# Attention of the last layer: other products take turns in the maxima's banks, q and k come in pieces of 256 tokens, polar pieces are dealt evenly

## The chip, the core and the metric

The kernel runs on one core of one Trainium2 chip. The time is device microseconds (us) of one execution. Five engines work side by side and meet at semaphores: TensorE (PE: matmuls, with its weight loads shown apart as PEld), VectorE (DVE), ScalarE (ACT), GpSimd (POOL) and SyncE (SP, which here only issues DMAs). Each runs its own instructions in the order in which the program gives them. PE writes its results to PSUM; the pools of this kernel divide it into eight banks of 128 x 512 float32.

## The reference

The program is a four-layer network over 2 sequences of 2048 tokens with 256 features. The change touches only the last layer:

```python
xn = _layernorm(x, axis=-1)
x = x + _L3_attn_ref(xn, Wq, Wk, Wv, Wo) + _L3_ffn_ref(xn, theta, phi, theta_noise, phi_noise)

# _L3_attn_ref: causal softmax attention, 16 heads of 16 features
scores = jnp.einsum('bhtc,bhkc->bhtk', q, k) * scale
scores = jnp.where(causal, scores, -jnp.inf)
attn = jax.nn.softmax(scores, axis=-1)
out = jnp.einsum('bhtk,bhkc->bhtc', attn, v)
return jnp.einsum('bsv,dv->bsd', out, o_proj_weight)

# _L3_ffn_ref ("polar"): length of a complex product
real = jnp.einsum('bti,io->bto', x, jnp.cos(theta + theta_noise))
imag = jnp.einsum('bti,io->bto', x, jnp.sin(phi + phi_noise))
return jnp.sqrt(real * real + imag * imag)
```

All of it is float32.

## The kernel before

The last layer is `layer3_attn`, with the polar part of sequence 0 done ahead of it by `layer3_ffn`. The 2 x 16 heads are cut into eight **groups** of four heads. A head has 16 features and takes a strip of 32 rows of the array, so that four heads' score matmuls stand in the four row strips together; a float32 matmul call shows in the profile as two matmul instructions. Each group goes through two passes over its scores. The *maxima pass* (`gm`, line 1380) computes q against k with queries on the partitions, and DVE takes the row maximum of each head (line 1401). The maxima are folded into a spare row of q (`fold`, lines 1234, 1240, 1242). The *exponential pass* (`ge`, line 1376) computes the scores again, transposed, with the maximum already subtracted; ACT takes the exponential (line 1390), POOL cuts the diagonal (1394), and PE multiplies by the values (1430, tile `ps_v`). `divide` scales by the row sums and `prod` multiplies by the output weights.

The order is written by hand, under a manual schedule. `waves` runs 40 **units** (tiles of 128 x up to 512 scores; 28 are 512 wide, four each 384, 256 and 128). It is called nine times:

- once for the maxima of group 0 alone (the *first maxima stage*),
- seven times for the exponentials of group n with the maxima of group n + 1 (the *joint stages*),
- once for the exponentials of group 7 alone (the *last stage*).

In a joint stage a unit consists of two **waves**; each has two score matmuls and two maxima matmuls, interleaved, e m e m. The value product of a unit ("held") is issued after the first wave of the next unit. In the other two stages a unit is one wave with all four heads, and a tile holds two heads in two banks.

Other work is put between units. `fill` is a list of steps in fixed order; `pieces` are products that become ready after a number of waves (`fold`'s transposes, `over` and `prod` of `divide`, the values of sequence 1); `steps` are the same without PE. After each unit (in a joint stage, after its second wave) one ready piece is taken, or else one fill step; and when as many fill steps are left as units, further ones are taken at once.

In the first maxima stage fill holds 53 steps. They are: values of sequence 0 (16), the polar part of sequence 1 in four blocks (for each: `stats` on ACT; `normed` on DVE and ACT; two `turned` transposes; four `product`s), and q and k of group 1 (8). With 53 steps and 40 units, 14 of them are taken at unit 0.

`qk` makes q and k of a group in four pieces of 512 tokens. A piece is two fill steps (`half`), one for each half of the 256 features; after the second, ACT copies the bank twice (line 1193 into the staging tile `qk`, which has one buffer; line 1194 into `qT`), and four DMAs on SP's queue (line 1196) move k's rows to their partitions in `kT`. For group 0 this runs bare, ahead of the first maxima stage.

The banks, eight in all:

| stage | banks before |
|---|---|
| first maxima stage | values 1 (`ps_v`, unused yet), other products 1 (`ps_p`), polar 2 (`ps_x`), maxima 2 double tiles (`ps_s`) |
| joint stages | `ps_v` 1, `ps_p` 1, scores 3 (`ps_e`), maxima 3 (`ps_m`) |
| last stage | `ps_v` 1, `ps_p` 1, scores 3 double tiles (`ps_s`) |

`f_tile` gives the one bank of `ps_p` to q and k, values, folds, `over` and `prod`. Line 68 is the helper `mm`, so that its products are told apart by their tiles (`ps_p<-w3b,xT` values, `ps_p<-w3b,se` output products, `ps_x<-cs,xT` polar products; line 1469 makes the polar transposes).

Of the kernel before, what the change touches and what calls it, by code (L numbers as in the profile page):

```python
# [14 lines left out]
F32 = mybir.dt.float32  # L15
# [8 lines left out]
P = 128  # L24
# [1077 lines left out]
def layer3_attn(g, tc, a, out):  # L1102
# [11 lines left out]

    nc = g.nc
    NQ = S // P
    with ExitStack() as es:
        wk = es.enter_context(tc.tile_pool(name="l3a", bufs=2))
        wb = None
        psv = es.enter_context(tc.tile_pool(name="l3v", bufs=1, space=bass.MemoryType.PSUM))  # L1120
        psf = es.enter_context(tc.tile_pool(name="l3p", bufs=1, space=bass.MemoryType.PSUM))
# [34 lines left out]
        def f_tile():  # L1156
            return psf.tile([P, 512], F32, name="ps_p", tag="f")
# [23 lines left out]
        def qk(G):  # L1181

            def half(n, k, st):
                def go():
                    if k == 0:
                        st["ps"] = f_tile()
                    nc.tensor.matmul(st["ps"], wqk[:, k, G.hg * P : (G.hg + 1) * P],  # L1187
                                     g.xT[:, k, G.b * S + n * 512 : G.b * S + (n + 1) * 512],
                                     start=k == 0, stop=k == 1)
                    if k == 1:  # L1190
                        c = slice(n * 512, (n + 1) * 512)
                        both = wk.tile([P, 512], F32, name="qk", tag="qk", bufs=1)
                        nc.scalar.copy(both, st["ps"])
                        nc.scalar.activation(G.qT[:, c], st["ps"], AF.Copy, scale=low16)
                        for j in range(4):
                            nc.sync.dma_start(G.kT[32 * j : 32 * j + 16, c], both[32 * j + 16 : 32 * j + 32, :])
                go.goes_on = k == 1
                return go

            fs = []  # L1200
            for n in range(4):
                st = {}
                fs += [half(n, 0, st), half(n, 1, st)]
            return fs
# [135 lines left out]
        def score_banks(both):  # L1340

            if both:
                pe3 = sc.enter_context(tc.tile_pool(name="l3e", bufs=3, space=bass.MemoryType.PSUM))
                pm3 = sc.enter_context(tc.tile_pool(name="l3m", bufs=3, space=bass.MemoryType.PSUM))
                return (lambda: pe3.tile([P, 1, 512], F32, name="ps_e3", tag="e"),
                        lambda: pm3.tile([P, 1, 512], F32, name="ps_m3", tag="m"))
            p2 = sc.enter_context(tc.tile_pool(name="l3s", bufs=3, space=bass.MemoryType.PSUM))
            return (lambda: p2.tile([P, 2, 512], F32, name="ps_s", tag="s"),) * 2

        def waves(ge, gm, fill, e_tile, m_tile):  # L1350
# [9 lines left out]
            for u in range(len(ue)):  # L1360
# [7 lines left out]
                for wave, (he, hm) in enumerate([((0, 1), (2, 3)), ((2, 3), (0, 1))] if both  # L1368
                                                else [((0, 1, 2, 3),) * 2]):
                    step = 1 if both else 2  # L1370
                    te = [e_tile() for _ in he[::step]] if ge else []
                    tm = [m_tile() for _ in hm[::step]] if gm else []
# [41 lines left out]

                    left = len(ue) - u
                    ready = [n for n, (when, f) in enumerate(pieces) if when <= now]
                    if ready and not (fill and (getattr(fill[0], "goes_on", False) or both and len(fill) >= left)):
                        pieces.pop(ready[0])[1]()
                    elif fill:
                        fill.pop(0)()  # L1420
                    while fill and len(fill) >= left:
                        fill.pop(0)()
                if ge:
                    def held(qb=qb, pts=pts, kt=kt, c0=c0):
                        nonlocal av
                        first, last = kt == 4 * qb, kt == (4 * qb - 1 if qb else 3)
                        if first:
                            av = psv.tile([P, 512], F32, name="ps_v3", tag="v")
# [12 lines left out]
        def polar(b):  # L1441

            fs = []
            for n in range(4):
# [3 lines left out]
                def stats(xb=xb, st=st):  # L1448
                    mv = st["mv"] = F.wk.tile([P, 3, 4], F32, name="mv3", tag="mv3")
# [41 lines left out]
        with tc.manual_schedule():  # L1491
            gs = [group(0), group(1)]
            for f in qk(gs[0]):
                f()
# [186 lines left out]
```

## Time and profile before

| | |
|---|---|
| median of 3 runs | 4361.61 us (4360.21 to 4363.71) |
| the profiled execution | 4356.61 us, its span 4354.9 us |
| PE busy | 3928.4 us, 90% of the span |
| DVE, ACT, POOL busy | 2544.0, 1954.2, 1278.9 us |
| bare q and k of group 0 | 2996.0 to 3012.2 us from the span's start |
| first maxima stage | 3012.2 to 3158.9 us |
| seven joint stages | 3158.9 to about 4240 us, some 154.4 us each |
| last stage and end | about 4240 to 4354.9 us |

The stages are read from the first and last starts of lines 1380 and 1376. In a line of a timeline the numbers are the start, in us from the span's start, and the duration; then engine, line, operation, and output tile <- input tiles, the shapes, and how many instructions were merged; in brackets stands the idle time of the engine before it and what ended it. In a line of the waits stand who waited, for whom, us in total, times, and the longest. The granted clock is the share of PE's full clock that the chip allowed in a stretch.

### The profile page before, as it was taken

To read this page: it belongs to the slowest core of one execution; us is meant where nothing else is said; L and a number is where in the kernel's file an instruction comes from. 1 tells how busy PE (TensorE), PEld (TensorE's weight loads), DVE (VectorE), ACT (ScalarE), POOL (GpSimd) and SP (SyncE) were. 2 spreads that over 40 slices of the span, in tenths; PEclk is the share of its full clock that TensorE was granted. 3 is DMA by queue.
4 is the path that set the end of the run, shared out by engine and by line. 5 is a ranking of instruction groups with operands and counts; after the bars stand their busy time and mean duration, and the time that the engine had idled before them with its cause. 6 is when DMAs were issued, how large, how long until landed. Compare 5 with 4: busy or idle time off the path is not lost.

```text
span 4354.9 us, 58086 instructions
## 1 busy us (share of the span) xinstructions
PE 3928.4 (90%) x21260; PEld 2297.7 (53%) x21260; DVE 2544.0 (58%) x6485; ACT 1954.2 (45%) x3713; POOL 1278.9 (29%) x1302
## 2 busy tenths in 40 slices
PE   6488988989879999999959999996999999999998
PEld 5356666766645555566536777673333333333332
DVE  6354444454378998999963322324666666666660
ACT  3234433343345555665422322324255555555556
POOL 1402222232166766656641111112111111101101
PEclk8687999999989999999979999998999999999999
DMA  4200222222345666666750000000000000000000
GB/s 179 91 32 32 73 70 79 79 79 80 128 119 186 219 199 208 212 211 216 223 180 1 1 1 1 1 1 25 4 8 8 5 4 16 16 9 9 4 2 26
DMA packets 106703, 330.18 MB, mean 76 GB/s; under 512 B 28561, under 2 KB 56866, under 8 KB 100018
## 3 DMA queue, kind: packets, MB, share of 16 engines
q0 software_dynamic: 52720, 264.15, 19.1%
q1 hardware_dynamic: 51234, 59.41, 4.2%
q8 instruction: 168, 2.75, 0.3%
q10 hardware_dynamic: 2464, 2.91, 0.2%
q14 instruction: 117, 0.96, 0.1%
HBM read 286.56 MB, written 33.03 MB: 73 GB/s over the span
## 4 chain that ended last, share of the span: by engine, by line
PE 53%; DVE 8%; DMA 3%; issue 2%; POOL 2%; ACT 1%; SPq 0%; ACTq 0%; DVEq 0%; POOLq 0%
PE ps_e L1376 12%; PE ps_v L1430 6%; PE ps_a L68 6%; PE ps_f L68 6%; PE ps_c L68 4%; PE ps_m L1380 3%; PE ps_k L68 2%; PE ps_p L68 2%; DMA G<-in_tab_in,ind 2%; PE ps_h L839 1%; DVE hid L817 1%; PE ps_o L1019 1%; PE ps_p L1187 1%; PE ps_s L1380 1%; PE ps_m L1384 1%
## 5 line engine op out<-in xcount | busy, mean ns | idle before, releaser
L1401 DVE TENSOR_REDUCE mp<-ps_m 128x1 f32<-128x512 f32 (+3 forms) x1120 | 632.1, 606 | 405.0 <-PE ps_m L1380 235.1
L1390 ACT ACTIVATE pt<-ps_e 128x512 f32<-128x512 f32 (+3 forms) x1120 | 537.9, 532 | 451.0 <-PE ps_m L1380 266.0
L1380 PE MATMUL ps_m<-kT,qT 32*128 32x512 f32 (+3 forms) x2240 | 677.2, 571 | 0.0
L1376 PE MATMUL ps_e<-qT,kT 32*128 32x512 f32 (+3 forms) x2240 | 656.0, 571 | 0.8 <-DVE mp L1401 0.5
L1376 PEld LDWEIGHTS ps_e<-qT,kT 32*128 32x128 f32 x2240 | 221.5, 183 | 354.9 <-issue 151.5
L1394 POOL TENSOR_SCALAR_AFFINE_SELECT pt<-pt 128x256 f32<-128x256 f32 x256 | 104.2, 408 | 857.6 <-ACT pt L1390 857.4
L805 POOL DMA_INDIRECT G<-in_tab_in,ind x256 | 273.8, 1070 | 213.8 <-DVE ind L792 63.8
L1430 PE MATMUL ps_v<-pt,vv 128*32 128x512 f32 (+3 forms) x2560 | 311.9, 541 | 1.6 <-POOL pt L1394 0.9
L805 POOL DMA_INDIRECT G<-in_tab_out,ind x256 | 268.1, 1047 | 85.5 <-issue 32.5
L68 PE MATMUL ps_e<-xgT,we 128*128 128x256 f32 x936 | 240.8, 404 | 27.0 <-ACT xgT L306 17.4
L68 PE MATMUL ps_f<-hb,l_b 128*128 128x512 f32 x1024 | 258.3, 404 | 0.0
L68 PE MATMUL ps_k<-wk,xt 128*128 128x512 f32 x512 | 255.0, 609 | 2.7 <-DVE ix L782 2.5
L1380 PEld LDWEIGHTS ps_m<-kT,qT 32*128 32x128 f32 x2240 | 226.6, 183 | 46.6 <-issue 41.0
L1009 ACT ACTIVATE hb<-ps_f 128x512 fp32r<-128x512 f32 x128 | 75.6, 597 | 313.6 <-PE ps_f L68 313.6
L68 PEld LDWEIGHTS ps_f<-hb,l_b 128*128 128x128 f32 x1024 | 190.2, 189 | 48.4 <-issue 6.7
L68 PEld LDWEIGHTS ps_e<-xgT,we 128*128 128x128 f32 x936 | 177.0, 198 | 70.2 <-ACT xgT L306 23.1
L834 DVE CUSTOM_DVE_ANT_0 scr<-hid,G,gate 128x512 f32<-128x512 f32 x256 | 200.3, 783 | 16.5 <-DMA G<-in_tab_out,ind 10.8
L1010 DVE SCALAR_TENSOR_TENSOR hb<-ps_f,hb 128x512 fp32r<-128x512 f32 x128 | 86.6, 684 | 211.0 <-ACT hb L1009 210.8
L494 DVE COPY_PREDICATED AT<-lm,ps_g 128x256 f32<-128x256 uint8 x224 | 104.7, 520 | 141.8 <-PE ps_g L489 141.8
L817 DVE SCALAR_TENSOR_TENSOR hid<-G,lin,hid 128x512 f32<-128x512 f32 x224 | 166.8, 745 | 2.0
L489 PE MATMUL ps_g<-qt,E 64*128 64x64 f32 x1792 | 137.5, 294 | 33.0 <-DVE E L485 24.3
L815 DVE CUSTOM_DVE_ANT_0 scr<-xn,G,gate 128x256 f32<-128x256 f32 x256 | 146.4, 572 | 34.4 <-DMA G<-in_tab_in,ind 33.6
(390 smaller groups left out, 7564.7 us busy)
## 6 DMA issues: line engine op xcount, KB each, us to landing
xgd<-zero SPq DMA_DIRECT2D x13, 768.0 KB, 12.7
xg<-xgd SPq DMA_DIRECT2D x39, 256.0 KB, 2.8
yd<-ye SPq DMA_DIRECT2D x39, 256.0 KB, 3.2
G<-in_tab_in,ind POOLq DMA_INDIRECT x256, 5.0
G<-in_tab_out,ind POOLq DMA_INDIRECT x256, 5.5
kT<-qk SPq DMA_DIRECT2D x128, 32.0 KB, 1.9
out<-x SPq DMA_DIRECT2D x8, 512.0 KB, 3.2
x<-in_x ACTq DMA_DIRECT2D x4, 512.0 KB, 9.3
```

The source lines that it names most:

```text
L68: nc.tensor.matmul(out, lhsT, rhs, start=(i == 0), stop=(i == n - 1))
L489: nc.tensor.matmul(two[r][:, n * 64 : (n + 1) * 64], E[r * 64 : (r + 1) * 64, n * P : (n + 1) * P], qt[r * 64 : (r + 1) * 64, n * 64 : (n ...
L494: nc.vector.copy_predicated(AT[:, r].rearrange("p e (n t m) -> p e n t m", t=2, m=m)[:, :, :, 1, :], lm[:, li * 64 : (li + 1) * 64].unsque ...
L805: nc.gpsimd.indirect_dma_start(G, None, a[tab], bass.IndirectOffsetOnAxis(ap=k.ind[:, h, j : j + 1], axis=0))
L815: nc.vector.tensor_tensor_reduce(scr[:, 0:D], k.xn[:, j, :], G[:, 0:D], k.gate[:, h, j : j + 1], 0.0, ALU.mult, ALU.add, lin[:, h : h + 1])
L817: nc.vector.scalar_tensor_tensor(hs, G[:, D:768], lin[:, h : h + 1], hid if h == 0 else hs, ALU.mult, ALU.add)
L834: nc.vector.tensor_tensor_reduce(scr, hs, G[:, 0:512], k.gate[:, h, j : j + 1], 0.0, ALU.mult, ALU.add, lout[:, h : h + 1])
L1376: nc.tensor.matmul(te[i // step][:, i % step, c0:512], ge.kT[row(j), kt * P : (kt + 1) * P], ge.qT[row(j), qb * 512 + c0 : (qb + 1) * 512] ...
L1380: nc.tensor.matmul(tm[i // step][:, i % step, 0:w], gm.qT[row(j), qi * P : (qi + 1) * P], gm.kT[row(j), ch * 512 : ch * 512 + w], start=Tr ...
L1390: nc.scalar.activation(pt[:, o : o + step, c0:512], te[i // step][:, :, c0:512], AF.Exp, scale=0.25)
L1401: nc.vector.tensor_reduce(gm.mp[:, qi, j : j + step, ch], tm[i // step][:, :, 0:w], AX.X, ALU.max, negate=True)
L1430: nc.tensor.matmul(av[row(j), c0:512], ge.vv[:, kt, row(j)], pts[j][:, c0:512], start=first, stop=last)
```

## The change

- **First maxima stage.** The pools for `ps_v` and `ps_p` are not open yet. All products but the maxima (q and k, values, folds, polar) share two banks (`ps_x`), and the maxima have three double tiles.
- **Deal of the fill.** `stats` is cut into four steps; the list becomes 68 steps in another order (polar steps alternate with values, then with the products of the block before); and in the stages with one pass they are dealt by proportion: after each unit, as many as bring the rest down to its share. A ready piece is taken besides.
- **Joint stages.** `ps_v` has one bank, scores three, maxima four. `f_tile` is the maxima's pool, so that q and k, values, folds, `over` and `prod` take the next of these four banks in turn.
- **q and k.** Eight pieces of 256 tokens, each a step of its own with both halves of the features; two staging buffers of half the size; eight times two ACT copies and eight times four DMAs a group.
- **Last stage.** As before: one bank for `ps_v`, one for the rest, three double tiles; the first two are opened anew.

```diff
-        psv = es.enter_context(tc.tile_pool(name="l3v", bufs=1, space=bass.MemoryType.PSUM))
-        psf = es.enter_context(tc.tile_pool(name="l3p", bufs=1, space=bass.MemoryType.PSUM))
+        psv = None
...
-        def f_tile():
-            return psf.tile([P, 512], F32, name="ps_p", tag="f")
+        f_tile = None
...
-            def half(n, k, st):
+            def piece(n):
                 def go():
-                    if k == 0:
-                        st["ps"] = f_tile()
-                    nc.tensor.matmul(st["ps"], wqk[:, k, G.hg * P : (G.hg + 1) * P],
-                                     g.xT[:, k, G.b * S + n * 512 : G.b * S + (n + 1) * 512],
-                                     start=k == 0, stop=k == 1)
-                    if k == 1:
-                        c = slice(n * 512, (n + 1) * 512)
-                        both = wk.tile([P, 512], F32, name="qk", tag="qk", bufs=1)
-                        nc.scalar.copy(both, st["ps"])
-                        nc.scalar.activation(G.qT[:, c], st["ps"], AF.Copy, scale=low16)
-                        for j in range(4):
-                            nc.sync.dma_start(G.kT[32 * j : 32 * j + 16, c], both[32 * j + 16 : 32 * j + 32, :])
-                go.goes_on = k == 1
+                    ps = f_tile()[:, 0:256]
+                    c = slice(n * 256, (n + 1) * 256)
+                    mm(nc, ps, [(wqk[:, k, G.hg * P : (G.hg + 1) * P],
+                                 g.xT[:, k, G.b * S + n * 256 : G.b * S + (n + 1) * 256]) for k in range(2)])
+                    both = wk.tile([P, 256], F32, name="qk", tag="qk", bufs=2)
+                    nc.scalar.copy(both, ps)
+                    nc.scalar.activation(G.qT[:, c], ps, AF.Copy, scale=low16)
+                    for j in range(4):
+                        nc.sync.dma_start(G.kT[32 * j : 32 * j + 16, c], both[32 * j + 16 : 32 * j + 32, :])
                 return go
...
+            return [piece(n) for n in range(8)]
...
+        def banks(name, bufs, shape=(P, 512)):
+            pool = sc.enter_context(tc.tile_pool(name=f"l3{name}", bufs=bufs, space=bass.MemoryType.PSUM))
+            return lambda: pool.tile(list(shape), F32, name=f"ps_{name}", tag=name)
...
                     left = len(ue) - u
                     ready = [n for n, (when, f) in enumerate(pieces) if when <= now]
-                    if ready and not (fill and (getattr(fill[0], "goes_on", False) or both and len(fill) >= left)):
+                    if ready and not (both and len(fill) >= left):
                         pieces.pop(ready[0])[1]()
-                    elif fill:
+                    elif fill and both:
                         fill.pop(0)()
-                    while fill and len(fill) >= left:
+                    while fill and not both and len(fill) > nf * (left - 1) // len(ue):
                         fill.pop(0)()
...
+            sc = ExitStack()
+            F.psum = f_tile = banks("x", 2)
             for f in qk(gs[0]):
                 f()
...
-            fill = [pl[0][0], *v[0:3], pl[0][1], *v[3:6], *pl[0][2]]
+            fill = []
+            for i in range(4):
+                fill += [pl[0][0][i], v.pop(0)]
+            fill += [pl[0][1], v.pop(0), v.pop(0), *pl[0][2]]
             for n in range(4):
-                a3 = pl[n + 1] if n < 3 else (None, None, [])
-                fill += [a3[0], *pl[n][3][0:2], *v[6 + 3 * n : 8 + 3 * n], a3[1], *pl[n][3][2:4],
-                         *v[8 + 3 * n : 9 + 3 * n], *a3[2]]
+                a3 = pl[n + 1] if n < 3 else ([None] * 4, None, [])
+                for i in range(4):
+                    fill += [a3[0][i], pl[n][3][i]]
+                fill += [*v[0:1], a3[1], *v[1:3], *a3[2]]
+                v = v[3:]
+            fill += v
             fill = [f for f in fill if f] + qk(gs[1])
...
+            waves(None, gs[0], fill, None, banks("s", 3, (P, 1024)))
+            sc.close()
...
-            tiles = score_banks(True)
+            v_tile = banks("v", 1)
+            tiles = banks("e", 3), banks("m", 4)
+            f_tile = tiles[1]
...
                 if n8 == 7:
                     sc.close()
-                    tiles = score_banks(False)
+                    v_tile, f_tile = banks("v", 1), banks("p", 1)
+                    tiles = banks("s", 3, (P, 1024)), None
```

## The prediction

> **What bounds the kernel now.** The page's first rows come first: of a span of 4354.9 us the matmul engine PE has 90%, and in the 40 slices the last layer's attention begins at about 2996 us. The change touches only what lies from there to the end, so I asked for the busy time by stretch, stage by stage (columns: stretch, us; busy us and instructions of PE, its weight loads, DVE, ACT, POOL; granted clock; DMA).
>
> ```profile
> 3016.00:3020.00 4.00, 1.24 (x3) 1.06 (x4) 0.34 (x2) 2.61 (x11) 0.00 (x0) 0.82 0.05 12
> 3020.00:3024.00 4.00, 3.08 (x7) 1.45 (x7) 0.00 (x0) 0.97 (x3) 0.00 (x0) 0.50 0.00 0
> 3024.00:3028.00 4.00, 3.08 (x9) 1.93 (x10) 0.00 (x0) 2.48 (x6) 0.00 (x0) 0.83 0.00 0
> ...
> 3012.00:3159.00 147.00, 132.36 (x577) 56.79 (x577) 84.84 (x94) 54.57 (x138) 22.56 (x25) 0.94 0.02 4
> 3159.00:3313.00 154.00, 153.73 (x1070) 52.86 (x1070) 95.29 (x174) 85.27 (x175) 14.70 (x37) 1.00 0.03 6
> 3622.00:3776.00 154.00, 152.09 (x1082) 53.22 (x1078) 94.26 (x174) 85.27 (x176) 22.36 (x43) 1.00 0.07 18
> 4240.00:4335.00 95.00, 92.92 (x680) 28.56 (x678) 4.61 (x11) 72.23 (x90) 20.39 (x38) 1.00 0.08 21
> ```
>
> PE looks full in every stage, but a PE that waits inside a wave is counted busy. So the waits come next: of the first maxima stage (3012 to 3159), then of the seven joint stages (3159 to 4240).
>
> ```profile
> DVE mp L1401 <- PE ps_s L1384: 39.1, 16, 17.1
> PEld ps_s L1380 <- DVE mp L1401: 36.1, 57, 1.8
> PE ps_s L1380 <- DVE mp L1401: 6.4, 13, 1.0
> ...
> PEld ps_e L1376 <- ACT pt L1390: 145.3, 244, 1.1
> PEld ps_m L1380 <- DVE mp L1401: 5.5, 23, 0.5
> ```
>
> In the first stage PE waits for maxima to leave their banks (36.1 + 6.4), and once DVE starves for 17.1 us. In the joint stages PE waits for exponentials, hardly for maxima. The timelines show how. First the end of the maxima stage:
>
> ```profile
> 3145.08 2.36 DVE L1401 TENSOR_REDUCE mp<-ps_s 128x2 f32<-128x1024 f32 x2 [0.36 <-PE ps_s L1380]
> 3145.83 1.12 PE L1187 MATMUL ps_p<-xT,w3a 128*128 128x512 f32 x2
> 3146.89 1.73 PE L1380 MATMUL ps_s<-kT,qT 32*128 32x512 f32 x8
> 3148.06 2.36 DVE L1401 TENSOR_REDUCE mp<-ps_s 128x2 f32<-128x1024 f32 x2 [0.63 <-PE ps_s L1380]
> 3148.55 1.12 PE L1187 MATMUL ps_p<-xT,w3a 128*128 128x512 f32 x2
> ```
>
> The eight score matmuls take 1.14 us when nothing blocks them, here 1.73: their second pair of heads waits for the second reduction of the unit before. A unit takes 2.7 to 3.0 us, with 2.13 of PE work and 2.36 of DVE work. Then a joint unit without another product:
>
> ```profile
> 3615.40 2.60 DVE L1401 TENSOR_REDUCE mp<-ps_m 128x1 f32<-128x512 f32 x4 [1.40 <-PE ps_m L1380]
> 3615.42 1.57 ACT L1390 ACTIVATE pt<-ps_e 128x512 f32<-128x512 f32 x3 [1.59 <-PE ps_m L1380]
> 3616.07 0.18 PEld L1376 LDWEIGHTS ps_e<-qT,kT 32*128 32x128 f32 x1 [0.71 <-ACT pt L1390]
> 3616.15 0.18 PEld L1380 LDWEIGHTS ps_m<-kT,qT 32*128 32x128 f32 x1
> 3617.20 0.16 PEld L1430 LDWEIGHTS ps_v<-pt,vv 128*32 128x32 f32 x8 [0.76 <-issue]
> ```
>
> Two waves follow each other directly from 3614.20; the fourth score tile waits for the exponential that empties the first of three banks (3616.07), the fourth maxima tile 0.08 longer for its reduction (3616.15), and the value product queued behind both starts at 3617.20. The unit lasts 4.00 us for about 3.1 of work. A unit with a product between the waves takes 4.2 and waits for nothing.
>
> **The first maxima stage** (146.7 us, from the first score matmul at 3012.17 to the first joint one at 3158.89). Before, 14 of 53 fill steps fall on unit 0, and the second unit starts only at 3038.97: 26.8 us, for 1.3 us of its own matmuls. After, 68 smaller steps are dealt at 1.7 a unit, and three double tiles stand in place of two.
> PE's work, from start to next start where it is not blocked: scores 28 x 1.07 + 4 x (0.86 + 0.65 + 0.43) = 37.7; masks 16 x 0.23 = 3.7; polar products 16 x 1.91 = 30.6; values 16 x 1.06 = 17.0; turns 8 x 0.57 = 4.6; q and k pieces 8 x 1.06 = 8.5; three folds 1.3. Sum 103.4.
> To it I add: (a) units in which DVE needs longer than PE. With the new deal unit by unit, the larger of the two sums to 109.8, which is +6.4 if nothing carries over; the third tile carries half a unit; I take 4. (b) A slow clock at the start. The rows above grant 0.82, 0.50, 0.83. Here the Trainium skill (TensorE: Matmul & The Clock Gate, Part 1) says that one busy window of about 3.4 us releases the clock, which would cost 1.7 us; its passage on PSUM-queue cycling says that short PE idles between groups bring the slow clock back, which speaks against dealing work round banks. The row of this stage agrees with the second, 0.94 over 147 us, against 1.00 in the joint stages with their idles of 0.8 us. By the first rule +1.7, at 0.94 throughout +6.6. The new stage is denser than the old; I take 3.5. (c) The polar chain: "normed" sits behind a DVE reciprocal that queues behind up to 2.4 us of reductions, then 2.07 us of ACT, and now only two value products (2.1 us, and a unit's scores, 1.07) stand between it and its transposes. Behind a waiting transpose queue all later scores. 0 to 2 us, four times: 4.
> (d) The q/k pieces at the end. Each issues four DMAs on SP; the trace shows four kT issues in 2.54 us, and rt<-se, a sixteenth of the size, also in 2.44, so the price is per DMA: eight pieces need 20.3 us of SP instead of 10.2. PE would bring them in about 14. With two buffers, piece 7's copy waits for piece 5's landing; its matmul waits for piece 5's bank: +2 on PE. ACT finishes its last copy some 4 us after PE's last piece, and the first exponentials, with their table load of 1.28, queue behind it on ACT: 4 us at the boundary, as score banks run out.
> Sum 103.4 + 4 + 3.5 + 4 + 2 + 4 = 120.9, **25.8 us less**. Ends: 109 (nothing but the larger sums of each unit: 38 less) and 137 (all of a to d doubled: 10 less).
>
> **Before it**, q and k of group 0 run bare: 16.15 us from 2996.02. There were four pieces, each waiting for the landing of the one before (4.6 to 5.1 us). After: piece 0's DMAs from about 2997.7, one piece per 2.54 us on SP; piece 5's copy needs piece 3 landed (2997.7 + 7.6 + 3.9 = 3009.2), piece 7's matmul follows at 3010, at half clock to 3012.1. That is where the first score matmul stood before (3012.17). I take 0, with 2 either way.
>
> **The joint stages.** The maxima get four banks, and the products lose their own. I went through the 280 places of the trace where one unit's second wave meets the next unit's first: 138 have no product between them. Where the last maxima matmul starts after the last score matmul, the fourth bank takes that lag away: 100 full-width junctions at 0.082 less the 0.007 of mere issue, 7.5 us; 38 masked ones at 0.165 (9), 0.317 (10), 0.183 (19), 7.9; waves behind a value product 1.5. That is 16.9, all serial on PE. More is not to be had: the score tiles keep three banks.
> A product in a maxima bank makes the tile four turns later wait for its reader. That is the last maxima tile of the next unit, which begins at least 1.3 us (narrow diagonal) and mostly 2.1 after the product; the reader (ACT copy 0.37 to 0.59, for q/k about 0.37 + 0.45, between the 0.40 of a 256-wide ACT pass and half of 0.694 more) sits behind two exponentials and ends 0.8 to 1.0 after it. I take 0.
> 48 pieces of four 256-wide matmuls take 1.06 each against 1.01 for a half of two 512-wide ones: +2.4. ACT gains 1.5 us a group (8 x 0.82 against 4 x 1.28), under 85 of 154 busy; without that cover it would be 9 us. SP's extra issues lie under 4 us per unit. Net **14.5 us less**; ends 0 and 20.
> The last stage keeps its pools (one, one, three double): 0.
>
> **Sum.** On the profiled execution, 4356.6 (span 4354.9) - 40.3 = 4316.3; it lies 5 under the median, so from the median 4361.6 - 40.3 = 4321.3, **4321**.
>
> **Rivals.**
> *Only the first stage gains* (0.18). For it: PE waits for maxima directly only 5.5 us in the joint stages; if the score waits take the slack, nothing is left but +2.4. 4361.6 - 25.8 + 2.4 = 4338.
> *The first stage is refused its gain* (0.09): the two fill banks, now shared by values, turns, products and q/k, and the DMA tail hold PE. Then it saves 10, and the joint stages 14.5: 4337.
> *It does not do what it says* (0.05): both gains eaten, within 0.2% (9 us, about what a measurement of this kernel can tell from no change): 4360.
> *Slower* (0.08). One mechanism: ACT reads the products late, and the maxima matmul behind the product's bank stops PE, in 143 units with a product. It costs x per unit; at x = 0.28 us the gain of 40 is gone, at 0.4 the time is 4321 + 57 = 4378. Against it: ACT and DVE are busy 55 to 62% of a joint stage, and the slack above is 0.4 to 1.1.
>
> **How the numbers follow.** The forecast has 0.60, with its own range 4303 to 4334. Faster: 0.60 + 0.18 + 0.09 = 0.87; same 0.05; slower 0.08. For 8 in 10 the range takes in the bounds of both parts and the two lesser gains: 4301 to 4346.
>
> **What would show it.** The stretch from the first score matmul to the first joint one falls from 146.7 to about 121, its clock over 0.94, DVE without the 17 us hole; line 1401's wait by the scores of that stage falls under 15 us. Joint stages go from 154.4 to about 152.3; the last maxima load starts within 0.02 us of the last score load. The step is wrong if PE waits in the joint stages for maxima banks released by ACT, or if ACT waits for kT landings by more than 8 us at the end of the first stage.

## The result, and the profile after

The changed kernel takes 4318.27 us, median of 4 runs (4312.33 to 4322.83), against 4360.91 us for the kernel before (4 runs on the same chip, 4356.2 to 4363.71). The ratio is 0.9903, with a 95% interval of 0.9885 to 0.992: 1.0% faster. The forecast was 4321.

Stage lengths, from the starts of the score and value matmuls in the two profiled executions:

| us | before | after | difference | predicted |
|---|---|---|---|---|
| bare q and k of group 0 | 16.15 | 16.42 | +0.3 | 0 |
| first maxima stage | 146.72 | 120.63 | -26.1 | -25.8 |
| seven joint stages | 1082.07 | 1065.94 | -16.1 | -14.5 |
| last stage and end | 113.95 | 113.93 | 0 | 0 |
| sum | | | -42.0 | -40.3 |

The spans of these executions (4354.9 and 4318.2 us) differ by only 36.7 us, because the layers ahead, which are the same code, ended 5.2 us later: q and k begin at 3001.24 after, at 2996.02 before. Over all the profiled executions told of here that start lies anywhere from 2993 to 3010 us, while the last stage, the same code in all of them, always takes 113.9 to 114.2. So the experiments are compared by stage lengths, and the times stand beside them. The lines shown from a view are those that the text needs; others between them are left out.

The profile after, busy time by stretch (columns: stretch, us; busy us and instructions of PE, its weight loads, DVE, ACT, POOL; granted clock; DMA share, GB/s):

```profile
3017.00:3021.00 4.00, 4.00 (x17) 1.76 (x17) 0.88 (x1) 0.92 (x3) 0.00 (x0) 0.56 0.10 25
3017.00:3138.00 121.00, 111.37 (x590) 52.53 (x589) 85.94 (x94) 55.95 (x148) 22.60 (x25) 0.97 0.02 6
3138.00:3142.00 4.00, 3.70 (x16) 1.63 (x18) 1.12 (x2) 2.61 (x4) 0.41 (x1) 0.50 0.12 29
3600.00:3754.00 154.00, 154.00 (x1112) 55.67 (x1114) 96.10 (x177) 88.48 (x188) 22.30 (x43) 1.00 0.07 18
```

The first maxima stage is the second row: DVE has nearly the same work as before (85.94 us against 84.84) in 26 us less, and the clock is 0.97, not 0.94. The third row has a price that was not in the sum: the joint stages begin at half clock.

The waits of the first maxima stage (3012 to 3139; who waited, for whom, us in total, times, longest):

```profile
DVE mp L1386 <- PE ps_s L1369: 25.6, 9, 18.5
...
PEld ps_s L1365 <- DVE mp L1386: 13.6, 20, 1.3
ACT xn L1451 <- DVE mv L1449: 8.1, 4, 2.2
```

The wait of the scores' weight loads for DVE (line 1386 is the reduction, 1401 before) fell from 36.1 to 13.6 us, that of the score matmuls themselves from 6.4 to 1.6. The 18.5 us in the first row is still there; what it is follows below. Among the waits of the joint stages (3139 to 4204), the one for exponentials is the largest on PE's side that a full bank causes:

```profile
PEld ps_e L1361 <- ACT pt L1375: 121.6, 235, 0.8
```

Before it was 145.3 us, in 244 places, up to 1.1. A joint unit without another product, in the timeline after (start, us; engine, line, operation; in brackets the idle time before and what ended it):

```profile
3591.85 0.18 PEld L1361 LDWEIGHTS ps_e<-qT,kT 32*128 32x128 f32 x1 [0.71 <-ACT pt L1375]
3591.86 0.18 PEld L1365 LDWEIGHTS ps_m<-kT,qT 32*128 32x128 f32 x1
...
3592.91 0.16 PEld L1416 LDWEIGHTS ps_v<-pt,vv 128*32 128x32 f32 x8 [0.76 <-issue]
```

The last score load and the last maxima load now stand 0.01 us apart (0.08 before), and the unit lasts 3.92 us instead of 4.00. The mean lag at the full-width places of this kind went from about 0.08 to under 0.01 us.

### The profile page after: what moved, and what is told of

The parts are those of the page before. It is cut to its first block, busy times and chain, and to the rows that moved or that the text cites. A ratio compares the mean times of both kernels' runs of the same rounds, so it can differ in the third digit from the quotient of the medians.

```text
span 4318.2 us, 58674 instructions
## 1 busy us (share of the span) xinstructions
PE 3903.7 (90%) x21388; PEld 2310.3 (54%) x21388; DVE 2546.8 (59%) x6485; ACT 1962.8 (45%) x3777; POOL 1278.5 (30%) x1302
## 3 DMA queue, kind: packets, MB, share of 16 engines
q0 software_dynamic: 52720, 264.15, 19.1%
## 4 chain that ended last, share of the span: by engine, by line
PE 53%; DVE 9%; DMA 3%; issue 2%; POOL 2%; ACT 1%; SPq 1%; ACTq 0%; DVEq 0%; POOLq 0%
PE ps_e L1361 12%; PE ps_v L1416 7%; PE ps_a L68 6%; PE ps_f L68 6%; PE ps_c L68 4%; PE ps_m L68 3%; PE ps_k L68 3%; PE ps_m L1365 2%; DMA G<-in_tab_in,ind 2%; DVE hid L817 2%; PE ps_o L1019 1%; PE ps_h L839 1%; PE ps_m L1369 1%; PE ps_x L68 1%; DVE scr L834 1%
## 5 line engine op out<-in xcount | busy, mean ns | idle before, releaser
L1365 PE MATMUL ps_m<-kT,qT 32*128 32x512 f32 (+3 forms) x2240 | 665.0, 573 | 0.0
L68 PE MATMUL ps_e<-xgT,we 128*128 128x256 f32 x936 | 242.0, 405 | 27.0 <-ACT xgT L306 17.2
L68 PE MATMUL ps_f<-hb,l_b 128*128 128x512 f32 x1024 | 258.8, 405 | 0.0
L68 PE MATMUL ps_k<-wk,xt 128*128 128x512 f32 x512 | 254.2, 607 | 3.0 <-DVE ix L782 2.7
L68 PEld LDWEIGHTS ps_f<-hb,l_b 128*128 128x128 f32 x1024 | 190.5, 189 | 48.4 <-issue 6.7
L68 PEld LDWEIGHTS ps_e<-xgT,we 128*128 128x128 f32 x936 | 177.5, 198 | 70.6 <-ACT xgT L306 22.8
```

Source lines behind the costliest of these rows:

```text
L68: nc.tensor.matmul(out, lhsT, rhs, start=(i == 0), stop=(i == n - 1))
L1365: nc.tensor.matmul(tm[i // step][:, i % step, 0:w], gm.qT[row(j), qi * P : (qi + 1) * P], gm.kT[row(j), ch * 512 : ch * 512 + w], start=Tr ...
```

## The experiments

Each kernel computes everything that the reference does. "Before" and "after" name the two kernels of this case. Stage lengths are given as bare q and k, first maxima stage, joint stages. Each ratio is to runs of the kernel before on the same chip (medians 4365.97, 4369.53 and 4362.43 us on the three chips used), so times of different chips are not to be subtracted.

| kernel | stages, us | time, us | ratio to before, 95% |
|---|---|---|---|
| pieces_alone | 20.23, 145.89, 1077.87 | 4363.68 | 0.9998 [0.9986, 1.0009] |
| joint_alone | 20.24, 146.23, 1062.88 | 4346.37 | 0.9955 [0.9942, 0.9967] |
| first_alone | 16.44, 120.61, 1079.24 | 4337.86 | 0.9937 [0.9916, 0.9957] |
| shared_three | 16.43, 120.65, 1121.67 | 4376.18 | 1.0024 [1.0017, 1.0032] |
| deal_alone | 21.79, 138.91, 1066.12 | 4345.71 | 0.9953 [0.9936, 0.9969] |
| third_tile_alone | 16.43, 121.58, 1065.44 | 4323.24 | 0.9895 [0.9878, 0.9911] |
| even_two_tiles | 16.43, 137.50, 1066.02 | 4337.13 | 0.9937 [0.992, 0.9954] |
| scores_four | 16.44, 120.69, 1081.63 | 4336.15 | 0.9935 [0.9918, 0.9952] |
| early_qk1 | 16.43, 115.45, 1063.61 | 4317.42 | 0.9887 [0.9871, 0.9904] |
| early_both | 6.71, 126.04, 1063.51 | 4317.96 | 0.9881 [0.9864, 0.9897] |
| norm_split | 16.43, 114.89, 1063.50 | 4311.27 | 0.988 [0.986, 0.99] |
| after_again | 16.43, 120.61, 1065.84 | 4322.86 | 0.9903 [0.9888, 0.9918] |

after_again is the changed kernel once more, on the chip of even_two_tiles, scores_four and norm_split.

> The changed kernel once more, on the same chip as norm_split, for comparison: first stage 120.6, joint stages 1065.9 us; norm_split 12 us below it (8 from the early pieces, 4 to 7 from the split).

Its stages repeat those of the first profile within 0.1 us, so stage differences of half a microsecond can be read.

### The parts one by one

**pieces_alone**: the kernel before, with the pieces of 256 tokens and nothing else.

```diff
-            def half(n, k, st):
+            def piece(n):
...
-            return fs
+            return [piece(n) for n in range(8)]
```

> The kernel before, with only q and k cut into eight pieces of 256 tokens (banks, list and deal of the first stage as before). My theory: the halves themselves bring nothing; 48 pieces at 1.06 instead of 1.01 us of PE cost 2.4 us in the joint stages, the bare q and k stay at 16 us, so about 4363 (4359 to 4368). Rival, that the finer pieces are what pays (two staging buffers, shorter ACT work): 8 to 15 us faster than the kernel before, 4346 to 4353.

**joint_alone**: pieces_alone, and in the joint stages four maxima banks that the products share. The first stage is as before.

```diff
-                pm3 = sc.enter_context(tc.tile_pool(name="l3m", bufs=3, space=bass.MemoryType.PSUM))
+                pm3 = sc.enter_context(tc.tile_pool(name="l3m", bufs=4, space=bass.MemoryType.PSUM))
...
+            f_tile = tiles[1]
```

> The kernel before with pieces of 256 and the new joint stages (scores three banks, maxima four, other products in turn with the maxima); the first stage keeps its banks, list and deal. My theory: the seven joint stages lose 16.9 us of waiting for maxima banks and pay 2.4 for the pieces: 4361 - 14.5 = 4346 (4341 to 4351). Rival, only the first stage gains: 4361 to 4364.

**first_alone**: the changed kernel with the old banks in the joint stages.

```diff
-            tiles = banks("e", 3), banks("m", 4)
-            f_tile = tiles[1]
+            tiles = banks("e", 3), banks("m", 3)
+            f_tile = banks("p", 1)
```

> The changed kernel with the joint stages' banks put back (values one, other products one, scores three, maxima three). My theory: the first stage's gain alone, 25.8 us, less 2.4 for the pieces: 4338 (4332 to 4344), and the joint stages as long as before, about 1082 us plus what the slow clock at their start costs. Rival, only the first stage gains: the whole 42 us stay, 4318 to 4322.

The two halves of the change add up, but for the clock where they meet. The fourth bank is worth 15.0 us (1077.87 to 1062.88), or 13.3 seen from the other side (1079.24 to 1065.94). On the other side the joint stages begin at half clock, for 8.5 us in the changed kernel and 4.5 in first_alone; in the first four units the changed kernel is 1.6 us behind first_alone, in all the others together 14.9 ahead. The pieces, alone, cost 4 us in the bare stretch (20.23 against 16.15) but make the joint stages 4.2 us *shorter*, where the sum had +2.4. What they saved stands in the trace of before, about 37 us into the second joint stage (and so in the fourth and sixth):

```profile
3349.71 2.40 SPq L1292 DMA_DIRECT2D se<-sv  x4
3353.54 0.73 PEld L68 LDWEIGHTS ps_p<-w3b,se 128*128 128x128 f32 x4 [2.44 <-DMA se<-sv]
```

Here `prod` waits for the DMAs that join the heads (`se<-sv`), and PE stands for 1.6 us; the waits of before have "PE ps_p L68 <- DMA se<-sv: 4.9, 3, 1.6", three such places. A second q/k half had to follow its first, and that pushed `over`, which issues these DMAs, to a later unit. With pieces there is no such rule, `over` comes earlier and the DMAs have landed: the line is gone, and that unit takes 4.20 us instead of 5.88. Three times 1.68 is 5.0, so the rest of the pieces' cost is +0.8. The time of pieces_alone is the one expected, about 4363, but for another reason: 4.1 us lost in the bare stretch and 4.2 won in the joint stages cancel.

**shared_three**: the products share the maxima's banks, but there are only three of these.

```diff
-            tiles = banks("e", 3), banks("m", 4)
+            tiles = banks("e", 3), banks("m", 3)
```

> The changed kernel with three maxima banks instead of four, the other products still in turn with them (one bank stays unused). My theory: sharing is free only because of the fourth bank. With three, the second maxima tile after a product needs the bank of the last tile before it, whose reduction ends about 0.37 us after the matmul could start; in 62 full-width units with a product that is 23 us, in the narrower ones up to another 15: 4338 + 23 to 38, that is 4361 to 4376. Rival, that the bank count doesn't matter and the shorter chain of pools does: 4318 to 4338.

Measured is more than expected: the joint stages take 42.4 us longer than with three banks and a separate one for the products (first_alone), and the kernel is slower than before. Its timeline, in a unit after a product:

```profile
3700.60 1.29 DVE L1386 TENSOR_REDUCE mp<-ps_m 128x1 f32<-128x512 f32 x2 [1.40 <-PE ps_m L1365]
...
3701.53 0.18 PEld L1361 LDWEIGHTS ps_e<-qT,kT 32*128 32x128 f32 x1 [0.33 <-ACT pt L1375]
3701.54 0.28 PEld L1361 LDWEIGHTS ps_e<-qT,kT 32*128 32x128 f32 x2
3701.94 0.29 PEld L1365 LDWEIGHTS ps_m<-kT,qT 32*128 32x128 f32 x2
3702.99 0.16 PEld L1416 LDWEIGHTS ps_v<-pt,vv 128*32 128x32 f32 x8 [0.76 <-issue]
```

The two maxima loads start at 3701.94, as soon as the second reduction is through (3700.60 + 1.29 = 3701.89), 0.4 us after the score loads; with four banks the lag was 0.01. Of the 42.4 us, 41 lie in the 143 units that follow a product. That is 0.30 a unit at the most, since up to 2 us belong to a longer half clock at the start (8.7 us against 4.5 in first_alone). With four banks the same 143 units are together 1.4 us shorter than in first_alone. So sharing is free only because there is a bank more; it is not free in itself.

**scores_four**: the fourth bank goes to the scores and the products share it there; three banks for the maxima.

```diff
-            tiles = banks("e", 3), banks("m", 4)
-            f_tile = tiles[1]
+            tiles = banks("e", 4), banks("m", 3)
+            f_tile = tiles[0]
```

> The changed kernel with the joint stages' banks the other way round: scores four, the other products in turn with them, maxima three. My theory: between two waves without a product the maxima tile waits 0.08 us longer than the score tile, so with maxima at three the fourth score bank brings nothing there: joint stages 1077 to 1081 us, as with separate banks (1079.2), 13 more than the changed kernel. Rival, that the score tiles' wait (145 us in all before) is the one that holds PE: 1060 or less.

The joint stages take 1081.63 us, 2.4 more than with three and three (1079.24); 2.0 of this lies in the first of them (156.27 against 154.29), and there in its first four units, where PE works at half clock for 8.7 us instead of 4.5; the second to the sixth agree within 0.1 us. The largest wait in the profile of before was for exponentials (145.3 us), and yet a bank for the scores gives nothing. That fits the two loads of the joint unit before (3616.07 and 3616.15): the maxima tile waited 0.08 us longer than the score tile, and the value product starts behind both.

### What makes the first stage shorter

The prediction led with the fill steps on unit 0. It and the description of the kernel count 14 of 53. The list has 56 (16 values, 32 polar steps, 8 halves of q and k), and 17 fall on unit 0: 13 with PE work stand between the first two units in the trace, besides two `stats` and two `normed`. Two runs took the deal and the third double tile apart, and a third one closed the gap between them.

**deal_alone**: the even deal, but two double tiles, and values and products on banks of their own.

```diff
-            F.psum = f_tile = banks("x", 2)
+            v_tile, f_tile = banks("v", 1), banks("p", 1)
+            F.psum = banks("x", 2)
...
-            waves(None, gs[0], fill, None, banks("s", 3, (P, 1024)))
+            waves(None, gs[0], fill, None, banks("s", 2, (P, 1024)))
```

> The changed kernel with the first stage's banks put back (two double tiles for the maxima, two polar banks, one for the other products), so that of the first stage only the even deal remains. My theory: the deal does away with the 26.8 us of unit 0, and the third tile only with the waits of the second pair of heads, 0.1 to 0.4 us in the units with little other work: first stage about 127 us instead of 120.6, 6 us over the changed kernel. Rival, that the third tile is the cause: 15 to 25 us over it.

**third_tile_alone**: the new banks, with the old list and the old deal (17 steps on unit 0).

```diff
-                    elif fill and both:
+                    elif fill:
                         fill.pop(0)()
-                    while fill and not both and len(fill) > nf * (left - 1) // len(ue):
+                    while fill and len(fill) >= left:
```

> The changed kernel with the old list and deal of the first stage (whole stats, 14 steps at unit 0) but the new banks (three double tiles, two banks for all else). My theory: the hole at unit 0 stays (about 26 us until the second unit), the 39 other units fall from 3.05 to about 2.65 us: first stage 130 us, 10 over the changed kernel. Rival, that the third tile is the cause: within 5 us of the changed kernel.

**even_two_tiles**: the changed kernel with one double tile fewer, nothing else.

```diff
-            waves(None, gs[0], fill, None, banks("s", 3, (P, 1024)))
+            waves(None, gs[0], fill, None, banks("s", 2, (P, 1024)))
```

> The changed kernel with two double tiles for the maxima of the first stage instead of three (two banks stay unused); the two shared banks for all else and the even deal remain. It parts what deal_alone put back together. Theory after the second set of runs: it is the third tile, since with two every unit's second pair of heads waits for DVE: first stage 134 to 139 us. Rival: it is the second bank for values and q/k, which in the kernel before had one: first stage 121 to 126 us and the bare q and k back to 16.4.

Both first expectations fell: deal_alone takes 138.91 us and not about 127, third_tile_alone 121.58 and not about 130. The third tile is worth 16.9 us at the even deal (137.50 to 120.63). With it in place, the even deal is worth 0.95 (121.58 to 120.63). At two tiles the even deal and the shared banks together give 8.4 us (145.89 in pieces_alone to 137.50), 1.4 of it by the sharing (138.91 in deal_alone). So deal and banks overlap, and the new banks alone, the third tile with the two shared ones, give nearly all. In third_tile_alone the second unit still starts 23.9 us after the first (3020.23 to 3044.12), and the other 39 take 97.7 us, 2.5 each: the steps on unit 0 were for the most part not waste. PE is busy for 17.4 of the 23.9 us, with work that has to be done somewhere, and while it runs no unit is held.

The timelines show what the tile does. First deal_alone, then the changed kernel, each a unit with the same polar product behind it:

```profile
3045.09 2.36 DVE L1386 TENSOR_REDUCE mp<-ps_s 128x2 f32<-128x1024 f32 x2 [0.94 <-PE ps_s L1365]
3045.26 1.98 PE L68 MATMUL ps_x<-cs,xT 128*128 128x512 f32 x4
3047.17 1.46 PE L1365 MATMUL ps_s<-kT,qT 32*128 32x512 f32 x8
3048.35 2.36 DVE L1386 TENSOR_REDUCE mp<-ps_s 128x2 f32<-128x1024 f32 x2 [0.90 <-PE ps_s L1365]
```

```profile
3112.71 2.36 DVE L1386 TENSOR_REDUCE mp<-ps_s 128x2 f32<-128x1024 f32 x2 [2.46 <-PE ps_s L1365]
3114.52 1.14 PE L1365 MATMUL ps_s<-kT,qT 32*128 32x512 f32 x8
3115.59 1.98 PE L68 MATMUL ps_x<-cs,xT 128*128 128x512 f32 x4
3115.69 2.36 DVE L1386 TENSOR_REDUCE mp<-ps_s 128x2 f32<-128x1024 f32 x2 [0.63 <-PE ps_s L1365]
```

With two tiles the engines take turns. The scores' second pair waits for the second reduction (1.46 us instead of 1.14), and DVE then idles 0.9 us until they are done: 3.26 us from one reduction to the next. With three tiles the scores take 1.14 and the units follow 2.98 us apart, PE's own work. The waits of the first stage say the same in sum, here of even_two_tiles:

```profile
PEld ps_s L1365 <- DVE mp L1386: 22.2, 34, 2.1
...
PE ps_s L1365 <- DVE mp L1386: 5.8, 14, 1.3
```

That is 28.0 us of waiting for DVE against 15.2 after (13.6 and 1.6): 12.8 of the 16.9.

The clock has a part in it, too. The first stage of even_two_tiles, then of deal_alone:

```profile
3011.88:3149.39 137.51, 125.63 (x590) 58.54 (x589) 86.20 (x94) 56.42 (x148) 22.57 (x25) 0.95 0.02 5
```

```profile
3018.13:3157.04 138.91, 121.52 (x590) 56.78 (x589) 86.20 (x94) 55.77 (x146) 22.58 (x25) 0.98 0.02 4
```

In this stage PE was at work at half clock for 15.9 us before, 13.3 in even_two_tiles, 6.3 in the changed kernel, 4.4 in deal_alone; half of that is the most it can have cost. So up to 4.8 of the 26.1 us came through the clock, and up to 3.5 of the third tile's 16.9. It can't stand in for the tile: deal_alone has less half clock than the changed kernel and takes 18.3 us longer. Smaller steps can't be told from it. The 7.0 us from pieces_alone to deal_alone, the even deal at two tiles, come with 17.9 us of half clock against 4.4, which can be worth 6.8.

The second shared bank has a use of its own. One bank for q and k makes the bare stretch 20.2 to 21.8 us (pieces_alone, joint_alone, deal_alone); with two it is 16.4 in every other kernel that runs these pieces bare.

### The end of the stage

**early_qk1**: the changed kernel, with q and k of group 1 spread over the stage instead of standing at its end.

```diff
-            fill = [f for f in fill if f] + qk(gs[1])
+            fill = [f for f in fill if f]
+            for n, f in enumerate(qk(gs[1])):
+                fill.insert(6 + 8 * n, f)
```

> The changed kernel with the eight q and k pieces of group 1 set evenly among the other fill steps instead of behind them. My theory: their 32 DMAs of 0.63 us on SP's queue and the last copies on ACT then lie under other work; the 5.05 us before the first joint score matmul shrink to about 1.1, PE doesn't idle there and the joint stage doesn't begin at half clock (3 us): 8 us below the changed kernel (5 to 11). Rival, that the boundary is the pools' turnover and the table load: within 2 us of the changed kernel.

The first stage falls by 5.2 us and the joint stages by 2.3, 7.5 in all; by the times alone (0.9887 against 0.9903 of before) it could not be told. In the changed kernel the end of the stage looks so:

```profile
3133.24 1.13 PE L68 MATMUL ps_x<-xT,w3a 128*128 128x256 f32 x4 [0.44 <-ACT qT L1190]
3134.86 0.37 ACT L1189 COPY qk<-ps_x 128x256 f32<-128x256 f32 x1 [1.67 <-DMA kT<-qk]
3137.50 0.37 ACT L1189 COPY qk<-ps_x 128x256 f32<-128x256 f32 x1 [1.89 <-DMA kT<-qk]
3138.30 1.22 PE L1361 MATMUL ps_e<-qT,kT 32*128 32x512 f32 x1 [3.92 <-ACT qT L1190]
```

ACT's copies wait for the landings of kT, SP's queue sets their pace (one piece in 2.5 us), and PE stands for 3.9 us before the first score. In early_qk1 that wait is 1.48 us, and the joint stages start at full clock. The stage also has no half-clock stretch like the one at 3082 us in the changed kernel (below), which is up to 1.7 of the 5.2 us.

**early_both**: besides, only two pieces of group 0 run bare; the other six are put among the first units.

```diff
-            for f in qk(gs[0]):
+            q0 = qk(gs[0])
+            for f in q0[0:2]:
                 f()
...
+            for n, f in zip((0, 2, 9, 11, 20, 22), q0[2:]):
+                fill.insert(n, f)
```

> As early_qk1, and of the q and k of group 0 only the first two pieces run bare; the other six are fill steps ahead of the units that read them. My theory: the bare stretch falls from 16.4 to about 6 us, of which some comes back as work in the first stage and as SP's pace in its first units: 6 to 9 us below early_qk1, 14 to 17 below the changed kernel. Rival, that the pieces' DMA pace moves into the first units and stops them: equal to early_qk1.

The bare stretch falls to 6.71 us, the stage grows to 126.04: together 132.7 against 131.9. Nothing is won, as the rival had it; the time moves into the stage. The six pieces bring 6.4 us of PE work with them (1.06 each). And PE waits 4.7 us for kT before the first score, just ahead of the stage, which then begins at half clock: in it PE works at half clock for 13.9 us against 3.1 in early_qk1, worth up to 5.4 of the 10.6 us that the stage is longer.

**norm_split**: early_qk1, with `normed` in two steps (the DVE part, and the ACT part some steps later) and another order of the steps around them, so that ACT does not wait for DVE. The first lines of its edit:

```diff
                     nc.vector.tensor_tensor(mv[:, 2, :], mv[:, 0, :], mv[:, 1, :], ALU.mult)
+
+                def scaled(xb=xb, st=st):
+                    mv, xn = st["mv"], st["xn"]
                     for i in range(4):
```

> As early_qk1, with the polar normalization cut in two steps (reciprocal on DVE first; the four scalings on ACT two steps later) and another order around it, so that ACT and PE have products between the reciprocal, the scaling and the transposes. My theory: ACT waits for DVE's queue there, values and transposes behind it wait for ACT, some 2 us in each of four places: first stage 115.5 to about 109 us. Rival: what is saved comes back as waits for DVE's reductions: 114 to 116 us.

The wait "ACT xn <- DVE mv" (11.3 us in early_qk1) is down to 0.7 us, and yet the stage falls only by 0.6 (115.45 to 114.89), not to the 109 expected. The wait was real, but hardly any of it lay on PE's path there. The rival's length came true, but not its reason: the score loads' wait for DVE is 12.8 us against 13.4. norm_split is the best version: 4311.27 us (4308.26 to 4319.8) against 4322.86 of after_again on the same chip, 0.988 against 0.9903 of before. Their intervals overlap a little ([0.986, 0.99] and [0.9888, 0.9918]); by the stages it is 8.1 us ahead, and 7.5 of these are early_qk1's. The rest of the 11.6 us between the medians has no place in the stages; the layers ahead, the same code, vary by more than that. So the 12 us expected were met by chance.

## Why the prediction was right, and where it was not

**The total** holds: 40.3 us predicted, 42.0 by stages, 42.6 by the medians. So do three of the signs: the clock of the first stage (0.97), the weight loads' wait there (13.6 us, under 15) and the mean joint stage (152.3 us).

**First stage, the size: right.** Predicted 120.9 us, measured 120.63 and 120.61. Of its terms: (b) the slow clock, 3.5 us. PE worked at half clock from 3017.7 to 3020.55 and from 3082.0 to 3085.4, 6.3 us, which costs 3.15 at most. The rule of the Trainium skill that was weighed as speaking against the change (TensorE: Matmul & The Clock Gate, its passage on PSUM-queue cycling) is not seen in the changed kernel: from 3021 to 3077 the clock is 1.00 in every stretch of 4 us, with products taking banks in turn, and in the joint stages, which cycle four of them, it is 1.00 too, once their start is over. In the kernel before it can't be ruled out: there the clock fell three times in the stage with little idling of PE ahead of it (last section). (d) 2 us on PE and 4 at the boundary: PE stood for 1.28 and 0.44 us between the last pieces and 3.92 before the first score, 5.6 us. But the sign that was named for it ("wrong if ACT waits for kT landings by more than 8 us") was badly chosen: ACT waits 11.3 us in six places there, while PE loses 5.6. (a) and (c), 4 us each, can't be read singly: the waits are 15.2 and 8.1 us, and they lie partly over each other and over PE's other work. Together they were given 8; what 103.4, 3.15 and 5.6 leave of the 120.6 is 8.4. The sum has one slip, in its upper end: with all of (a) to (d) doubled it is 138, not 137.

**First stage, the reason: half wrong.** The working led with 14 steps on unit 0 (there are 17) and "26.8 us, for 1.3 us of its own matmuls". That is not the loss: PE is busy for 19.1 of these 26.8 us, and third_tile_alone keeps such a stretch and 25.1 of the 26.1 us gain. The sum came out right because it was made of PE's work and not of the parts' gains, so it didn't matter which part freed PE. The clock was in the sum as a price only; that up to 4.8 us of the gain came through it was not foreseen. "Once DVE starves for 17.1 us" was a misreading as well. The wait is still there after, 18.5 us, and its place is the bare q/k stretch before the first maxima, in which DVE has nothing to reduce. The hole of unit 0 is in another row of the waits of before, in which the reciprocal of `normed` ends it:

```profile
DVE mv L1460 <- ACT mv L1456: 18.6, 2, 16.1
```

The forecast of a DVE "without the 17 us hole" failed for that reason. A longest wait has to be looked up by its place before it is put down to one.

**Joint stages: right in mechanism, two terms off and one left out.** The fourth bank gave 15.0 us for the 16.9 predicted; the lag at full-width junctions fell to under 0.01 us, as forecast (within 0.02). The pieces gave 4.2 us where the sum had cost them at +2.4; the step that failed is the one that priced only their matmuls, and not the order of the steps behind them. Left out was the half clock at the start: 2.3 us against early_qk1, 3.1 against joint_alone, whose joint stages also begin at full clock. With the latter, -15.0 - 4.2 + 3.1 = -16.1. That the total came within 1.6 us of the forecast is in part luck: the pieces were off by 6.6 us one way, the fourth bank and the clock by 5.0 the other. No wait of PE for a maxima bank that ACT releases appears among the joint stages' waits. Weight loads of products wait for DVE to free such a bank (41.0 us in 54 places, up to 0.8, with no such row for PE's matmuls); whether the missing 1.9 of the fourth bank's 16.9 lies there was not separated. "More is not to be had: the score tiles keep three banks" was too narrow: scores_four shows that a fourth score bank in place of the maxima's would not have been more either.

**The slower rival** needed a late reader at 0.28 us in 143 units. With four banks no such wait is seen. With three, shared_three pays up to 0.30 a unit and ends at 1.0024, on the other side; there it is not ACT that is late (its copies hold a maxima load for 0.8 us in all), but DVE's reduction, one bank too near.

**Bare q and k**: predicted 0, measured +0.3. The reason, two buffers and the SP queue, is incomplete: without the second shared bank it would have been +4.

## What to carry to other kernels

Where a producer and a consumer of nearly equal pace share two buffers, the first gain to look for is a third buffer: here it was 17 of 26 us, and the deal of the other work brought 1 once it was there. When two users share a rotating pool, count the turns: here with one bank more it was free, without it it cost some 0.3 us at each use. And a stage's length was well predicted here as the sum of the bound engine's own work plus its pauses, though the reason given for the gain was half wrong; a gain put down to one ugly-looking stretch needs a run that keeps this stretch and takes the rest away.

## What the runs showed of the hardware

**The clock changes on a raster.** Read in steps of half a microsecond, the granted clock of the changed kernel falls at 3010.3, 3082.0 and 3136.6 us and comes back at 3020.5, 3085.4 and 3146.8. All these lie on one raster of 3.41 us. The stretch round the second fall:

```profile
3078.50:3080.50 2.00, 0.10 (x1) 0.00 (x0) 2.00 (x2) 2.00 (x5) 0.00 (x0) 1.00 0.00 0
3080.50:3082.00 1.50, 1.29 (x12) 0.73 (x12) 0.06 (x1) 1.01 (x3) 0.00 (x0) 1.00 0.00 0
3082.00:3085.50 3.50, 3.50 (x18) 1.61 (x12) 2.36 (x2) 1.59 (x5) 0.00 (x0) 0.51 0.00 0
3085.50:3088.00 2.50, 2.50 (x16) 0.97 (x12) 1.88 (x2) 0.00 (x0) 0.00 (x0) 1.00 0.02 7
```

PE stood from 3078.60 to 3080.71 behind a late `normed`. It was at work again for 1.3 us when the clock fell, and one raster step later it came back. So this pause of 2.1 us cost 2.1 and then up to 1.7 more. The Trainium skill (TensorE: Matmul & The Clock Gate, Part 1) gives the same free-running window, 3413 ns, and one busy window for the return; by its table a whole idle window is needed for the fall. Here less was enough: 2.1 us of idling in the window, and 2.3 in the one that ended at 3136.6; a pause of 1.28 us (before 3130.60) left the clock at 1.00. No bound follows from this. The kernel before fell to half clock after windows with 1.3, 1.0 and 0.7 us of idling (at 3052.7, 3069.7 and 3103.9), and third_tile_alone stayed at 1.00 after one with 1.9. The last of the three, then third_tile_alone, each with the window that follows:

```profile
3100.46:3103.88 3.42, 2.69 (x14) 0.60 (x8) 3.17 (x5) 0.53 (x2) 0.00 (x0) 1.00 0.00 0
3103.88:3107.29 3.41, 3.41 (x6) 1.17 (x4) 1.80 (x2) 1.54 (x4) 0.00 (x0) 0.50 0.00 0
```

```profile
3037.09:3040.50 3.41, 1.48 (x5) 0.41 (x3) 0.34 (x2) 3.31 (x13) 0.00 (x0) 1.00 0.00 0
3040.50:3043.90 3.40, 3.40 (x12) 2.17 (x12) 0.00 (x0) 2.18 (x6) 1.41 (x2) 1.00 0.00 0
```

In the first of these windows score matmuls wait inside their wave for DVE (2.47 us from 3101.96, 1.14 where nothing blocks them), and this counts as busy; whether that is what the clock saw was not tested.

**The return can take longer.** At the boundary the clock stayed at 0.50 from 3136.6 to 3146.8, three raster steps, though the profile shows no pause of PE after 3138.5. Why one full window was not enough there stays open. That is the half clock that the joint stages paid with 2 to 3 us, and early_qk1, with a pause of 1.48 us, did not pay.

**Half the size, the same time.** The profile after, in its list of DMA issues, has the pieces' kT transfers at 1.8 us from issue to landing for 16 KB; for the halves of 32 KB it was 1.9. Four of them are issued in 2.43 us (at 3162.38), and four of twice the size took 2.43 before (at 3179.35). At the end of the first stage ACT's copies follow each other at this pace, 2.53 us apart on the mean (3127.38 to 3137.50, four steps). So at these two sizes the price is per DMA, as the prediction had it:

```profile
kT<-qk SPq DMA_DIRECT2D x256, 16.0 KB, 1.8
```
